# Layer 1's convolution in a four-layer network: six products of 128 columns for four tokens instead of four products of 256 columns for two tokens

## The chip, the cores and the metric

The program runs on one core of a Trainium2 chip. The core has a matrix engine (TensorE, PE in the profile, with its weight loads listed apart as PEld), a vector engine (VectorE, DVE), an engine for activation functions (ScalarE, ACT), a general engine (GpSimd, POOL) and an engine that here does nothing but issue transfers (SyncE, SP). The engines run side by side, each works through its own instructions in the order in which they were put there, and they wait for each other by semaphores. Sixteen DMA engines move data between the device's memory and the core's.

The metric is the time of one execution on the device in microseconds (us). Three runs of the kernel before took 4932.82, 4935.36 and 4935.79 us; the median is 4935.36 us.

## The reference

Two sequences of 1024 tokens with 1024 channels go through four layers, each an attention-like part and a feed-forward part, and after each of these eight parts the input is added and the rows are normalized. All is float32. The change is in the attention part of layer 1, which begins with a convolution over three neighbouring tokens:

```python
x = lax.conv_general_dilated(inputs, conv_w, window_strides=(1,), padding='SAME',
                             dimension_numbers=('NWC', 'WIO', 'NWC')) + conv_b   # 1024 -> 768 channels
q, k, v = jnp.split(x, 3, axis=-1)                # 256 channels each, blocks of 128 tokens
qh = jnp.einsum('btd,dhe->bthe', q, wq) + bq      # 16 heads of 64; kh and vh likewise
scores = jnp.einsum('bqhe,bkhe->bhqk', qh * scale, kh)   # causal within the block
p = jax.nn.softmax(scores, axis=-1)
o = jnp.einsum('bhqk,bkhe->bqhe', p, vh)
o = jnp.einsum('bqhe,hed->bqd', o, wo) + bo
return o.reshape(N, L, W_) @ proj_w + proj_b
```

Written out, the output at token t is W0·x(t−1) + W1·x(t) + W2·x(t+1) + b, with three 1024×768 matrices W0, W1, W2.

## The kernel before, in words

The two sequences (batches) are worked through one after the other, and in each the four layers in turn. `x` holds the rows, `xT` their transposed copy, 8 channel blocks (`k`) of 128 partitions, with one column of zeros ahead of token 0 and one behind token 1023. Weights go through one pool of eight buffers of 128×1024 floats (`self.w()`, tag `w`, 512 KB each); PSUM has eight banks of 512 columns (`self.ps()`).

**The convolution** is done for the two halves `th` of 512 tokens, and in each for six groups `co` of 128 output channels. It uses the identity that yields two neighbouring outputs from four products instead of six. With `j` the number of the product, the moving operand is a sum or a difference of two columns of `xT` (d2+d1, d2−d1, d0−d2, d3−d1), the stationary one is a matrix made of the weights (W0+W1+W2, W0−W1+W2, W0, W2). Each product covers 256 columns (each second token of the half) and sums over 8 channel blocks: 8 matmuls of 128×128 weights and 256 columns. One matmul of float32 stands in the profile as two records, one PEld and one PE each. So a half has 6 × 4 × 8 = 192 matmuls, 384 records, at line 666 (`call(j, k)`).

- `sums(eng, th, ks, outs)`, whose instructions stand at line 631, makes the moving operands. For the first half VectorE does it, into `qh` and `kh` (free until the heads are computed); for the second half GpSimd does it, into the columns of `xT` that the first half no longer needs.
- `load()` at line 647 fetches a group's weights. The made matrices are made only once, in batch 0's first half, by three VectorE instructions on 128×1024 floats (lines 651, 652, 655), and stored to memory (`cvd`, line 657, issued by SP); later they are loaded from there.
- ScalarE copies products 0 with the bias (line 672, `ce`), VectorE adds and subtracts product 1 (line 679, `cf`) and `last()` (line 682) joins these with products 2 and 3 into `qkv`, whose columns of one parity are two apart.

**The first half** of each batch overlaps the end of layer 0: tiles 4 to 7 of `x` still wait for layer 0's feed-forward result, which is loaded from memory as `ys` (line 709) and added by `add_y` (eight PE transposes, line 149; VectorE adds, line 157, and statistics, lines 168 and 169), normalized (`ln_roots`, lines 176 to 188, and `ln_scale`, line 191) and transposed into `xT` by `to_xT` (eight PE transposes, line 135; copies by VectorE, line 102, and ScalarE, line 104, in turn). The order of all this, with groups 0 and 1, is written out by hand in a block `with self.tc.manual_schedule():`, where each engine takes its instructions in the order of the program text. Groups 2 to 5 stand behind that block, and there a scheduler orders the instructions. Then the heads of the first half are computed (`heads(0, ...)`, line 109 in the profile).

**The second half's** convolution is dealt out over the attention of the first half: `attend(calls, per, units)` works on 8 units (4 blocks × 2 groups of heads) in 10 steps, and between the parts of a step it issues `per` entries of the list `calls`, which holds the 192 matmuls, the loads, the joins and eight `add_row` (GpSimd, line 142). `per` is 27.

Of the kernel before, what the change touches and what calls it, by code (L numbers as in the profile page):

```python
# [8 lines left out]
F = mybir.dt.float32  # L9
# [18 lines left out]
class Net:  # L28
# [7 lines left out]
    def __init__(self, ctx, tc, ins, out):  # L36
# [31 lines left out]
        self.cb2 = c.tile([P, 6], F, name="cb2")  # L68
# [523 lines left out]
    def l1_attn(self, b, yd, op):  # L592
        nc, i = self.nc, self.i
        row = self.row("l1_projb")
        with self.tc.tile_pool(name=self.nm("l1a"), bufs=1) as lp, self.tc.tile_pool(name=self.nm("l1s"), bufs=2) as spool:
# [18 lines left out]
            u0 = lp.tile([P, HALF], F, name=self.nm("u0"))  # L614
            cb2 = self.cb2
            if b == 0:
                self.cvd = self.dp.tile([6, 2, P, D], F, name=self.nm("cvd"))
# [5 lines left out]
            def sums(eng, th, ks, outs):  # L623
                v = [
                    self.xT[:, ks, th * HALF + o : th * HALF + o + HALF].rearrange("p k (i s) -> p k i s", s=2)
                    for o in (0, 2)
                ]
                d = [v[j // 2][:, :, :, j % 2] for j in range(4)]
                for j, o in outs:
                    x, y, op = ((2, 1, ALU.add), (2, 1, ALU.subtract), (0, 2, ALU.subtract), (3, 1, ALU.subtract))[j]  # L630
                    eng.tensor_tensor(o, d[x], d[y], op)

            def moving(th, j, k):
                cs = slice(256 * (j % 2), 256 * (j % 2) + 256)
                if th == 0:
                    return (qh, kh)[j // 2][:, k, cs]
                if j // 2:
                    return self.xT[:, k, 1 + cs.start : 1 + cs.stop]
                if k == 0:
                    return u0[:, cs]  # L640
                return self.xT[:, k - 1, 1 + HALF + cs.start : 1 + HALF + cs.stop]

            def conv(th, co):
# [3 lines left out]
                def load():  # L647
                    g = [self.w(i["l1_conv"][co, 0])]
                    if b == 0 and th == 0:
                        g1, g2, t = self.w(i["l1_conv"][co, 1]), self.w(i["l1_conv"][co, 2]), self.w()  # L650
                        nc.vector.tensor_tensor(t, g[0], g2, ALU.add)
                        nc.vector.tensor_tensor(t, t, g1, ALU.add)
                        if co == 0:
                            sums0(0)
                        nc.vector.scalar_tensor_tensor(g1, g1, -2.0, t, ALU.mult, ALU.add)
                        for n, f in enumerate((t, g1)):
                            nc.sync.dma_start(self.cvd[co, n], f)
                        w["w"] = [t, g1, g[0], g2]
                    else:
                        es = [self.w(self.cvd[co, n]) for n in range(2)]  # L660
                        w["w"] = es + g + [self.w(i["l1_conv"][co, 2])]

                def call(j, k):
                    if k == 0 and j % 2 == 0:
                        w["p", j // 2] = self.ps()
                    nc.tensor.matmul(  # L666
                        w["p", j // 2][:, 256 * (j % 2) : 256 * (j % 2) + 256], w["w"][j][:, k * P : (k + 1) * P],
                        moving(th, j, k), start=k == 0, stop=k == KD - 1,
                    )
                    if (j, k) == (2, 1):  # L670
                        w["e"] = spool.tile([P, 256], F, tag="ce", bufs=1, name=self.nm("ce"))
                        nc.scalar.activation(w["e"], w["p", 0][:, :256], AF.Identity, bias=cb2[:, co : co + 1])
                    if (j, k) == (2, 4):
# [20 lines left out]

            c0, c1 = conv(0, 0), conv(0, 1)
            with self.tc.manual_schedule():
                c0[0]()  # L700
                if b:
                    sums0(0)
# [1571 lines left out]
```

## Time and profile before

The table is made from the profile's views by stretch of time; a stage runs from the first to the last of its work on the chain of waits.

| stage | us from the span's start | length | records of line 666 | busy PE | busy VectorE | busy GpSimd |
|---|---|---|---|---|---|---|
| whole program | 0 to 4929.1 | 4929.1 | 1536 | 4529.3 | 3288.3 | 2176.1 |
| batch 0, first half | 294.2 to 407.0 | 112.8 | 384 | 97.78 | 57.94 | 26.84 |
| batch 0, second half, in the attention | 447.6 to 563.2 | 115.6 | 384 | 114.71 | 30.55 | 35.09 |
| batch 1, first half | 2755.6 to 2854.8 | 99.2 | 384 | 92.78 | 35.27 | 19.59 |
| batch 1, second half, in the attention | 2896.0 to 3011.0 | 115.0 | 384 | 114.11 | 30.54 | 35.09 |

The profiled execution took 4930.85 us; its span, from the first instruction of the program to the last, is 4929.1 us. That is 4.5 us below the median of the three timed runs.

How to read it: the four stages with the convolution are 443 us, 9% of the span. In the two second halves PE is busy nearly all the time. In the first halves it is not: there are times at which it waits for VectorE. In batch 0 the made weights are made as well, and that first half takes 13.6 us longer than batch 1's.

### The profile page before, as it was taken

To read this page: it belongs to the slowest core of one execution; us is meant where nothing else is said; L and a number is where in the kernel's file an instruction comes from. 1 tells how busy PE (TensorE), PEld (TensorE's weight loads), DVE (VectorE), ACT (ScalarE), POOL (GpSimd) and SP (SyncE) were. 2 spreads that over 40 slices of the span, in tenths; PEclk is the share of its full clock that TensorE was granted. 3 is DMA by queue.
4 is the path that set the end of the run, shared out by engine and by line. 5 is a ranking of instruction groups with operands and counts; after the bars stand their busy time and mean duration, and the time that the engine had idled before them with its cause. 6 is when DMAs were issued, how large, how long until landed. Compare 5 with 4: busy or idle time off the path is not lost.

```text
span 4929.1 us, 50567 instructions
## 1 busy us (share of the span) xinstructions
PE 4529.3 (92%) x16968; PEld 2231.8 (45%) x16968; DVE 3288.3 (67%) x4421; ACT 2012.2 (41%) x4065; POOL 2176.1 (44%) x1341
## 2 busy tenths in 40 slices
PE   9989989988888888999999999799888988899999
PEld 4357646433333333564443676464333333335644
DVE  5552267399999998545365422653999999976453
ACT  2521232377765654122025212334776756531310
POOL 2132112088888986130021321211888889850310
PEclk9999999999999999999999999999999999999999
DMA  2153212488888999411122532123888899983100
GB/s 92 54 182 131 75 66 90 130 221 228 238 217 230 249 247 248 159 51 48 52 69 63 182 111 71 58 67 122 216 222 236 211 241 256 250 265 120 63 13 30
DMA packets 285256, 723.89 MB, mean 147 GB/s; under 512 B 36928, under 2 KB 87232, under 8 KB 284996
## 3 DMA queue, kind: packets, MB, share of 16 engines
q1 hardware_dynamic: 277316, 695.47, 49.5%
q0 software_dynamic: 7680, 25.17, 1.5%
q8 instruction: 136, 2.23, 0.2%
q14 instruction: 124, 1.02, 0.1%
HBM read 607.00 MB, written 94.63 MB: 142 GB/s over the span
## 4 chain that ended last, share of the span: by engine, by line
PE 55%; DVE 18%; DMA 10%; issue 4%; POOL 4%; ACT 3%; SPq 1%; DVEq 0%; POOLq 0%; ACTq 0%
PE ps L109 15%; DVE h L1385 9%; PE ps L666 6%; PE ps L1757 4%; PE ps L2067 4%; DMA h<-dxd 3%; PE ps L1493 3%; POOL h L1371 2%; PE ps L1770 2%; DVE h L1396 2%; PE ps L1711 2%; PE ps L1407 2%; PE ps L135 2%; PE ps L1378 2%; DMA xi<-xcd 1%
## 5 line engine op out<-in xcount | busy, mean ns | idle before, releaser
L1371 POOL TENSOR_TENSOR h<-h,br 128x1024 f32<-128x1024 f32 x512 | 1205.5, 2370 | 106.6 <-DMA h<-dxd 63.7
L1378 PE MATMUL ps<-hl,rep 128*128 128x512 f32 x1024 | 731.9, 719 | 180.5 <-DVE h L1385 144.6
L1380 ACT ACTIVATE ps<-ps,l_Alog 128x512 f32<-128x512 f32 x1024 | 662.3, 662 | 550.7 <-PE ps L1378 548.0
L1385 DVE TENSOR_TENSOR_SCAN h<-ps,hst,h 128x512 f32<-128x512 f32 x512 | 633.9, 1284 | 20.8 <-ACT ps L1380 17.6
L1396 DVE TENSOR_TENSOR h<-h,ps 128x1024 f32<-128x1024 f32 x512 | 617.3, 1206 | 1.5 <-ACT hst L1393 1.4
L1385 DVE TENSOR_TENSOR_SCAN h<-ps,h 128x512 f32<-128x512 f32 x512 | 599.0, 1211 | 18.8 <-ACT ps L1380 18.8
L1493 PE MATMUL ps<-xT,w 128*128 128x512 f32 x1024 | 548.3, 622 | 8.8 <-DVE h L1385 7.6
L1378 PEld LDWEIGHTS ps<-hl,rep 128*128 128x128 f32 x1024 | 200.9, 197 | 608.3 <-DVE h L1385 436.7
L142 POOL TENSOR_TENSOR x<-x,row 128x1024 f32<-128x1024 f32 x80 | 191.3, 2410 | 548.7 <-PE ps L135 522.5
L1407 PE MATMUL ps<-h,sel 128*32 128x512 f32 x2048 | 294.9, 628 | 5.9 <-DVE h L1396 5.9
L1531 PE MATMUL ps<-w,w 128*128 128x512 f32 x512 | 275.5, 622 | 21.3 <-DMA w<-yd 18.7
L830 POOL TENSOR_TENSOR s<-s,l1r 128x512 f32<-128x512 f32 x64 | 66.5, 1039 | 489.1 <-DVE l1r L829 448.1
L1493 PEld LDWEIGHTS ps<-xT,w 128*128 128x128 f32 x1024 | 190.3, 195 | 203.4 <-issue 166.3
L1316 POOL TENSOR_TENSOR e<-e,one 128x512 f32<-128x512 f32 x64 | 81.5, 1273 | 446.3 <-ACT xp L1188 314.0
L1438 PE MATMUL ps<-xT,w 128*128 128x512 f32 x512 | 271.5, 629 | 6.1 <-DVE h L1385 6.1
L157 DVE TENSOR_TENSOR x<-x,ps 128x512 f32<-128x512 f32 x192 | 128.8, 683 | 216.6 <-PE ps L2073 136.2
L1196 DVE SCALAR_TENSOR_TENSOR ps<-xp,l_convw,ps 128x512 f32<-128x512 f32 x192 | 145.1, 756 | 186.3 <-ACT ps L1191 181.8
L1757 PE MATMUL ps<-w,w 128*128 128x512 f32 x512 | 229.4, 595 | 0.0
L2067 PE MATMUL ps<-w,xT 128*128 128x512 f32 x512 | 225.9, 593 | 0.0
L109 PE MATMUL ps<-xT,w 128*128 128x512 f32 x512 | 225.1, 592 | 0.0
L182 ACT ACTIVATE rs<-mv 128x1 f32<-128x1 f32 (+2 forms) x72 | 14.7, 204 | 473.1 <-DVE mv L176 472.7
L135 PE MATMUL ps<-ident,x 128*128 128x128 f32 x1024 | 140.6, 290 | 58.3 <-DVE x L191 53.4
(300 smaller groups left out, 7748.8 us busy)
## 6 DMA issues: line engine op xcount, KB each, us to landing
h<-dxd SPq DMA_DIRECT2D x512, 512.0 KB, 7.9
w<-l_in SPq DMA_DIRECT2D x128, 512.0 KB, 6.3
w<-l_out SPq DMA_DIRECT2D x96, 512.0 KB, 8.3
w<-l_conv SPq DMA_DIRECT2D x54, 512.0 KB, 4.1
w<-cvd SPq DMA_DIRECT2D x36, 512.0 KB, 3.4
w<-l_fw SPq DMA_DIRECT2D x32, 512.0 KB, 6.2
xcd<-xo SPq DMA_DIRECT2D x64, 256.0 KB, 6.2
xi<-xcd SPq DMA_DIRECT2D x64, 256.0 KB, 8.8
```

The source lines that it names most:

```text
L109: self.nc.tensor.matmul(out, lhsT, rhs, start=j == 0, stop=j == n - 1)
L666: nc.tensor.matmul(w["p", j // 2][:, 256 * (j % 2) : 256 * (j % 2) + 256], w["w"][j][:, k * P : (k + 1) * P], moving(th, j, k), start=k == ...
L1371: nc.gpsimd.tensor_tensor(hs[k], hs[k], norms[of(k)[0]][1].unsqueeze(1).to_broadcast([P, 2, HALF]), ALU.mult)
L1378: nc.tensor.matmul(dA[k, m], rep[:, 4 * m + q, :], hl[u, c][:, jj, :], start=True, stop=True)
L1380: nc.scalar.activation(dA[k, m], dA[k, m], AF.Exp, scale=A[:, g : g + 1])
L1385: nc.vector.tensor_tensor_scan(hs[k][:, m, :], dA.pop((k, m)), hs[k][:, m, :], hst[:, g : g + 1] if u else 0.0, ALU.mult, ALU.add)
L1396: nc.vector.tensor_tensor(hs[k], hs[k], norms[of(k)[0]][3].unsqueeze(1).to_broadcast([P, 2, HALF]), ALU.mult)
L1407: nc.tensor.matmul(py[u, c][32 * j : 32 * j + 32, :], self.sel[:, q, :], hs[k - 1 + j // 2][:, j % 2, :], start=False, stop=q == 3,)
L1493: nc.tensor.matmul(p, w["w"][:, k * P : (k + 1) * P], self.xcols(k, u * HALF, HALF), start=k == 0, stop=k == KD - 1)
L1531: nc.tensor.matmul(p, y[:, cc, t * P : (t + 1) * P], wt[:, cc * HALF : (cc + 1) * HALF], start=c2 == 0 and cc == 0, stop=last,)
L1757: nc.tensor.matmul(pa[tt], y[:, cc * HALF + tt * P : cc * HALF + (tt + 1) * P], w[:, cc * HALF : (cc + 1) * HALF], start=c2 == 0 and cc == ...
L2067: nc.tensor.matmul(p, self.xcols(k, tt * P, P), wt[k][:, ns], start=k == 0, stop=False)
```

## The change

The change replaces the identity for two outputs by the one for four: from six products come four neighbouring outputs (where the direct way needs twelve). A product now covers each fourth token of the half, 128 columns; a half has 6 × 6 × 8 = 288 matmuls of 128 columns instead of 192 of 256.

- **Moving operands**: twelve VectorE instructions on 128×1024 floats (or their parts) per half, with operands that lie four columns apart in `xT`; also for the second half, where GpSimd did it before. They go to `qh`/`kh` for the first half, and to `xT`'s first 768 columns and `vh` for the second.
- **Weights**: six matrices per group; products 0 and 5 use W0 and W2 as they are, products 1 to 4 use made matrices. In batch 0's first half they are made by six VectorE instructions per group, each ahead of the product that needs it (`make`), and stored by GpSimd's queue. W0 and W2 are fetched twice there, once for the making (`raw`) and once for products 0 and 5. So that stage issues 5 loads and 4 stores per group (before: 3 and 2), and the other three stages 6 loads per group (before: 4).
- **Loads as buffers come free**: `queue` lists the loads in order, `pump()` issues those whose buffer (the eighth before them) has been given up by an instruction already written, and each product's last matmul calls it.
- **Joining**: per group two ScalarE copies of 128 columns, and on VectorE two instructions of 256 columns and six of 128 columns, the last four behind product 5 (before: one ScalarE copy and two VectorE instructions of 256 columns, one of 512 columns). The factor −1/6 that the identity leaves is put into the scales of the heads, whose instructions stay as many.
- **Order**: the whole first half, groups 2 to 5 too, is now in the hand-written block. In batch 1 groups 0 and 1 go product by product in turn; in batch 0 group 0 comes first, then group 1. The `sums` of the second half are placed behind products of groups 3 and 4. In `attend`, `per` becomes 36, and the list has 288 matmuls.

The diff, cut to its core:

```diff
-            def sums(eng, th, ks, outs):
...
+            def spot(th, j):
+                if th == 0:
+                    t, n = {1: (qh, 0), 2: (qh, 1), 3: (qh, 2), 4: (qh, 3), 0: (kh, 0), 5: (kh, 1), "a": (kh, 2),
+                            "b": (kh, 3), "c": (kh, 2), "e": (kh, 1)}[j]
+                    return t[:, :, n * P : (n + 1) * P]
...
+            def sums(th, steps, k0=0, k1=KD):
...
+                    if m in (1, -1):
+                        nc.vector.tensor_tensor(o, q, p, ALU.add if m > 0 else ALU.subtract)
+                    else:
+                        nc.vector.scalar_tensor_tensor(o, p, float(m), q, ALU.mult, ALU.add)
+            one = [(2, d[2], -4, d[4]), ("a", d[1], -4, d[3]), (1, "a", 1, 2), (2, "a", -1, 2)]
+            two = [(4, d[2], -1, d[4]), ("b", d[1], -1, d[3]), (3, "b", 2, 4)]
+            c_, e_ = ("c", d[2], -1, d[0]), ("e", d[3], -1, d[5])
+            three, five = [(0, "c", 4, 4), (4, "b", -2, 4)], [(5, "b", -4, "e")]
+            def pump():
+                while queue and (len(ring) < WB or ring[-WB] in freed):
+                    key, f = queue.pop(0)
+                    ring.append(key)
+                    f()
...
+                def raw():
+                    for name, j, src in (("g0", "r", 0), ("g2", 1, 2), ("t", 2, None), ("n", 3, None), ("g1", 4, 1)):
...
+                def make(j):
+                    if j == 1:
+                        nc.vector.tensor_tensor(w["t"], w["g0"], w["g2"], ALU.add)
+                        nc.vector.scalar_tensor_tensor(w["g0"], w["g2"], 4.0, w["g0"], ALU.mult, ALU.add)
+                    w[j] = w[{1: "g2", 2: "t", 3: "n", 4: "g1"}[j]]
+                    if j < 3:
+                        nc.vector.tensor_tensor(w[j], w["t"], w["g1"], ALU.add if j == 1 else ALU.subtract)
                     else:
+                        nc.vector.scalar_tensor_tensor(
+                            w[j], w["g1"], 2.0 if j == 3 else -2.0, w["g0"], ALU.mult, ALU.add
+                        )
+                    nc.gpsimd.dma_start(self.cvd[co, j - 1], w[j])
+                    if j == 4:
+                        free((th, co, "r"))
...
                 def call(j, k):
+                    if k == 0 and j in (1, 0):
+                        w["p", j == 0] = self.ps()
                     nc.tensor.matmul(
+                        part(j), w[j][:, k * P : (k + 1) * P], spot(th, j)[:, k, :], start=k == 0, stop=k == KD - 1
                     )
+                    if k == KD - 1:
+                        free((th, co, j))
...
+                def early():
+                    w["e"] = spool.tile([P, 256], F, tag="ce", bufs=1, name=self.nm("ce"))
+                    nc.scalar.activation(w["e"][:, :P], part(1), AF.Identity, bias=cb6[:, co : co + 1])
+                    nc.scalar.copy(w["e"][:, P:], part(3))
+                def middle():
+                    f = spool.tile([P, 4, P], F, tag="cf", bufs=2, name=self.nm("cf"))
+                    for n, op in enumerate((ALU.add, ALU.subtract)):
+                        nc.vector.tensor_tensor(
+                            f[:, 2 * n : 2 * n + 2, :].rearrange("p a b -> p (a b)"), w["e"], w["p", False][:, 2 * P :], op
+                        )
...
+                    nc.vector.scalar_tensor_tensor(w["q"][:, 1, :], s4, -0.5, s2, ALU.mult, ALU.add)
+                    nc.vector.tensor_tensor(w["q"][:, 2, :], a1, a3, ALU.subtract)
+                def last():
+                    a1, a3, s2, s4 = w["f"]
+                    nc.vector.scalar_tensor_tensor(a1, part(0), -1.5, a1, ALU.mult, ALU.add)
+                    nc.vector.scalar_tensor_tensor(w["q"][:, 0, :], a3, -0.25, a1, ALU.mult, ALU.add)
+                    nc.vector.scalar_tensor_tensor(s2, part(5), -6.0, s2, ALU.mult, ALU.add)
+                    nc.vector.scalar_tensor_tensor(w["q"][:, 3, :], s4, -2.0, s2, ALU.mult, ALU.add)
...
+            ORDER = (1, 2, 3, 4, 0, 5)
+            def product(co, j):
+                if b == 0 and 1 <= j <= 4:
+                    c[co]["make"](j)
+                c[co]["calls"](j)
+            def root(tt):
+                self.ln_roots([tt])
+                self.ln_scale(tt)
             with self.tc.manual_schedule():
...
+                if b == 0:
+                    c[0]["make"](1)
+                for k0, k1 in ((0, 2), (2, 4), (4, KD)):
+                    sums(0, one, k0, k1)
+                    c[0]["calls"](1, k0, k1)
...
+                else:
+                    product(0, 0)
+                    product(0, 4)
+                    c[0]["both"]()
+                    self.table()
+                    self.add_y(4, ys)
+                    root(4)
+                    product(1, 1)
+                    self.add_y(5, ys)
+                    product(1, 2)
+                    self.to_xT(4)
+                    product(1, 3)
+                    sums(0, [e_] + five)
+                    product(1, 0)
+                    product(1, 4)
+                    c[1]["both"]()
+                root(5)
+                for j in (1, 2, 3):
+                    product(2, j)
+                self.add_y(6, ys)
+                for co in (0, 1):
+                    product(co, 5)
+                    c[co]["last"]()
...
+                later = {
+                    (3, 2): [lambda: self.to_xT(7)], (3, 3): [lambda: sums(1, [c_] + one)], (3, 5): [lambda: sums(1, two)],
+                    (4, 2): [lambda: sums(1, [e_])], (4, 4): [lambda: sums(1, three + five)],
+                }
+                for co in (3, 4, 5):
+                    for j in ORDER:
+                        product(co, j)
+                        if j == 0:
+                            c[co]["both"]()
+                        for f in later.get((co, j), []):
+                            f()
+                    c[co]["last"]()
...
-                attend(calls, 27, [(tt, g) for tt in range(4) for g in range(2)])
+                attend(calls, 36, [(tt, g) for tt in range(4) for g in range(2)])
```

`both()` is `early()` and then `middle()`. In the second half `early()` stands behind the first matmul of product 4 and `middle()` behind the third matmul of product 0; `last()` of a group follows the second matmul of the next.

## The prediction

> **What bounds the kernel now.** I read the times of the stages first, then the chain of waits inside them, then the single rows. The chain (start, length, what, how many records) in batch 0:
>
> ```profile
> 351.51 55.49 PE ps L666 x256
> 407.00 41.20 PE ps L109 x96
> ...
> 454.95 10.57 PE ps L666 x48
> 465.51 0.46 PE ps L795 x2
> 465.97 1.09 PE ps L801 x16
> 467.06 2.79 PE ps L666 x12
> 469.85 0.87 PE ps L837 x8
> 470.73 3.89 PE ps L666 x18
> 474.62 1.03 PE ps L848 x16
> ```
>
> Groups 2 to 5 of the first half (256 records) and the whole second half are TensorE alone: no piece of another engine stands between. A unit of attention puts L795, L801, L837 and L848 on that chain, 0.46 + 1.09 + 0.87 + 1.03 = 3.45 us, 27.6 for eight units. So in a second half every matmul record counts. The timeline shows the records' cost:
>
> ```profile
> 448.58 0.97 PEld L801 LDWEIGHTS ps<-kh,qh 64*128 64x128 f32 x16 [0.35 <-issue]
> 448.59 1.16 PE L801 MATMUL ps<-kh,qh 64*128 64x128 f32 x16
> 450.00 3.00 PEld L666 LDWEIGHTS ps<-xT,w 128*128 128x128 f32 x14
> 450.21 3.19 PE L666 MATMUL ps<-xT,w 128*128 128x256 f32 x14
> ```
>
> One 256-column record of L666 lasts 0.38 us, but fourteen take 3.19: (3.19 − 0.38) / 13 = 0.216 us each, the weight load hidden under the record before.
>
> The first half of batch 0 begins in the hand-ordered block, and there VectorE sets the pace:
>
> ```profile
> 308.06 1.23 DVE L651 TENSOR_TENSOR w<-w,w 128x1024 f32<-128x1024 f32 x1 [5.61 <-DMA w<-l_conv]
> 309.32 1.23 DVE L652 TENSOR_TENSOR w<-w,w 128x1024 f32<-128x1024 f32 x1
> 310.58 1.23 DVE L655 SCALAR_TENSOR_TENSOR w<-w,w 128x1024 f32<-128x1024 f32 x1
> 311.73 2.36 DVE L631 TENSOR_TENSOR kh<-xT 128x1024 f32<-128x1024 f32 x2
> 313.00 0.93 PEld L666 LDWEIGHTS ps<-kh,w 128*128 128x128 f32 x3 [5.83 <-DVE kh L631]
> ```
>
> TensorE wants the sums of L631 and has to wait 5.8 us because group 1's weights, which nobody needs yet, stand ahead of them on VectorE. The block keeps the text's order, and each instruction on 128×1024 floats costs 1.23 us.
>
> **The matmuls.** A half has 288 matmuls of two records, 576 records of 128 columns, instead of 384 of 256. The trace has no record with 128×128 float32 weights and 128 columns that is not a transpose. From below: half of 0.216 is 0.108; the transposes of L837 take 0.87 / 8 = 0.109. From above: a load that hides under nothing adds as much again, 0.216. Nearest is L801: ordinary float32 records, 128 columns, loads as wide as the convolution's, in two row groups that work side by side, so sixteen are eight steps: (1.16 − 0.27) / 8 = 0.111. I take 0.112: 576 × 0.112 = 64.5 us per half, against 384 × 0.216 = 82.9.
>
> The Trainium skill speaks against this, "TensorE: Matmul & The Clock Gate": its section "LDWEIGHTS (loading the stationary operand)" puts a load at its columns / 1.2, 107 ns here, "Weight-path perf modes" excludes float32 from fast loads, and "The mechanism" lets a load overlap a running matmul only in another row group. By that rule a record would cost its own 0.108 plus 0.107, and the matmuls would gain nothing: 576 × 0.215 = 124 us per half. The rows of L666 contradict the last part of it, since their loads hide in the same row group; whether one still hides when the matmul is as short as the load, no row shows for 128 rows.
>
> **The second halves** (115.6 and 115.0 us before). TensorE after: 64.5 + 27.6 = 92.1. Beside it lie the joins: VectorE gets 2.4 us per group instead of 1.5 (256 columns 0.34 to 0.41 by L679's row, 128 columns about 0.28 by L428's 0.269; two and six), 14 us in all where it was busy 30 of 115; ScalarE's two copies (L819's kind, 0.37 each) replace one of 0.47. GpSimd's eight `add_row` (2.4 each) run ahead of the attention as before: the first four fill it until about 15 us into the stage, and the weights of unit 1 that stand behind them are needed at 28. Loads: 36 × 0.524 MB = 18.9 MB in 95 us, 199 GB/s, and single slices of the page show 265. Before, 115.6 − 82.9 − 27.6 = 5.1 us were waits and seams, 2.8 of them in the tail behind the last join (VectorE, GpSimd, copy; 558.6 to 563.2 on the chain). With 36 entries per step the list reaches into the last steps and hides some: I keep 3. 92.1 + 3 = 95, **−20 us each, −40 for both**; −16 to −22 with waits between 1 and 5 and a record between 0.109 and 0.116.
>
> **Batch 1's first half** (99.2). No weights are made. Products 64.5, 64 transposes × 0.109 = 7.0. Waits, walked through in the block's order: 4.7 at the start (four sums on two channel blocks, 1.4 us, ahead of the first matmul, then as many and then twice as many ahead of the later ones of product 1), 1.8 until `ys` has landed at 2772.7 (fixed by layer 0's last scatter), 2.0 until tile 7 is normalized: 8.5. VectorE has 65 us of work and is behind TensorE only there. 80 us, **−19**. Six loads in a group's 10.75 us are 293 GB/s; the stretch 2757 to 2773 moved 305, the stretch 312 to 322 363, so the loads stay hidden; without that cover each group costs up to 1.1 us more (3.15 MB at 265 GB/s, 11.9), 6 in all. Range −13 to −21.
>
> **Batch 0's first half** (112.8) is where the change costs. VectorE's own list: making 36 × 1.23 = 44.3; sums of both halves 24 at 1.23, 30.1 with the first four in parts; joins 6 × 2.4 = 14.4; four `add_y` × 2.73 (two adds, two statistics, 0.21); four roots and scales × 2.48; four copies × 0.67. Together 112, against 57.9 now, and it is laid in one order with the products. Column by column:
> - Groups 0 to 2: VectorE works 67.4 us (22.1 making, 15.3 sums, 7.2 joins, 10.9, 9.9, 2.0) and waits six times for a product or a transpose written just ahead of its next instruction (1.9 to 5.2, together 21.3): 88.7.
> - Group 3: 3.7 for `make(1)` (three instructions) while TensorE stands still, 2.4 for the next two, 4.6 waiting for tile 7's transposes, copy 0.7, five sums 6.2, `make(4)` 1.2, 3.6 until product 4 is through, 1.25, three sums 3.7, 1.2: 28.6.
> - Groups 4 and 5: `last()` waits for product 5, and `make(1)` of the next group stands behind it: 3.7 + six products 10.75 + 0.6 + 1.7: 16.8 each.
>
> Sum 151. The 1.7 is the clock: the trace's clock record grants TensorE half speed from 296.7 to 303.5, 310.4 to 317.2 and 330.9 to 334.3, pieces of 3.4 us, each around or behind a wait of 3 us or more (the mean was 0.77 to 312 and 0.74 to 322). Nine of the waits here are longer than that; with half speed for 3.4 us after each the stage is 151, at full speed 137. Two us come on top at the start, because `g1` is now the fifth buffer and so behind a scatter of layer 0 (median 7.4 us to landing). I take 150, **+37**, range +22 to +55.
>
> What else moves there: GpSimd's sums (26.8 us busy) are gone, and 24 stores on its queue at about 1.0 (L499's indirect issues, the nearest row) lie beside nothing. SP issues 30 loads instead of 18 and no stores; each waits for its buffer, and `ys` stands behind the first eight entries, as before. 54 transfers are 28.3 MB in 150 us, 189 GB/s. A group's `g2` may be fetched only once `make(4)` of the group before has read `g0`; it lands 4.1 us later and is needed 8 to 12 us later in groups 3 to 5, some 3 us later in group 2, so it costs at most 2.
>
> **Sum**: −40 − 19 + 37 = −22 on a span of 4929.1: 4907. The timed runs lie 6.3 above the span (median 4935.4), so **4913**.
>
> **Rivals.**
> - *The making hides.* Before, groups 2 to 5 of batch 0 ran without a wait though their weights were made meanwhile. If the block let VectorE make ahead, this half would fall like batch 1's: 113 − 19 = 94, sum −78, 4857. Against: the order shown at 308 to 313. 0.10.
> - *The weight load shows.* Place: every record of a product. If a record takes over about 0.125 us nothing is left: each 0.001 costs 1152 × 0.001 in the second halves and some 0.6 us in the first, 1.8 together, so 22 us are gone at 0.112 + 0.012. At 0.216 the second halves last 155 (+39 each), batch 1's first 135 (+36), batch 0's 200 (+87): +201, 5136. For it: a load's row lasts 0.189 us. Against: L801's loads last 0.188 too (its stretch of 0.97 holds sixteen) and follow each other at 0.11. 0.10.
> - *Batch 0 eats it all*, if its first half takes 162 to 182 by loads that land late: within 10 us of before. 0.13. Beyond 182 slower: 0.08.
>
> **How the numbers follow.** A measurement of this kernel tells 0.2%, 10 us, from no change. The forecast has 0.59, its own range 4890 to 4925 (bounds of the three terms, not all at once). Faster: 0.59 + 0.10 = 0.69; within 0.2%: 0.13; slower: 0.10 + 0.08 = 0.18. The range 4885 to 4942 leaves out most of the first rival and of the second.
>
> **What would show it.** The product line's records start every 0.11 us and last 0.27; the second halves take about 95 us with TensorE alone on the chain; batch 1's first half 80; batch 0's 150, with waits of 4 to 9 us of TensorE that end on VectorE's `w`, and a granted clock under 0.9. I am wrong if the records stand at 0.13 or more, if TensorE waits for loads of `w` (`cvd`, `l_conv`) in batch 1, or if batch 0's first half is under 130.

## The result and the profile after

| | runs | median us | lowest to highest | span of the profiled run |
|---|---|---|---|---|
| before | 6 | 4935.57 | 4932.82 to 4940.27 | 4929.1 |
| after | 6 | 4954.69 | 4948.66 to 4959.43 | 4952.6 |

After to before: 1.0039, 95% interval 1.0027 to 1.0051. The change costs some 19 us; 4913 was predicted, with a range of 4885 to 4942. The result is outside it and on the other side.

Where it went, by stage. A first half is counted from the last transpose of tokens 0 to 511 to the first matmul of the heads, a second half from the last matmul of the heads to the first of the output projection (0.3 us more or less, as the start or the end of that last matmul is taken):

| stage | before | after | measured | predicted |
|---|---|---|---|---|
| batch 0, first half | 112.9 | 166.4 | +53.5 | +37 |
| batch 0, second half | 115.2 | 101.7 | −13.5 | −20 |
| batch 1, first half | 98.9 | 88.3 | −10.6 | −19 |
| batch 1, second half | 115.2 | 101.7 | −13.5 | −20 |
| the four together | 442.2 | 458.1 | +15.9 | −22 |
| all else | 4486.9 | 4494.5 | +7.6 | 0 |

All four signs are as predicted, and all four sizes are off to the bad side. "All else" is code that the change doesn't touch, but 5.9 of its 7.6 us come from the change all the same (see e5); in the six profiles without that effect it takes between 4486.9 and 4507.6 us, so the other 1.7 are not read as an effect. From here on kernels are compared by their stages, and by the timed ratio where there is one.

The stages of after in the view by stretches of time (stretch, length, then busy time and number of records of PE, PEld, VectorE, ScalarE and GpSimd, the granted clock of TensorE, the busy share of the DMA engines, GB/s):

```profile
296.40:462.80 166.40, 99.46 (x641) 96.24 (x642) 113.43 (x161) 8.91 (x26) 14.68 (x25) 0.75 0.54 186
504.00:605.50 101.50, 96.78 (x914) 89.27 (x912) 41.75 (x97) 29.84 (x147) 35.22 (x24) 1.00 0.61 199
2799.70:2888.60 88.90, 78.09 (x645) 76.68 (x644) 71.71 (x125) 17.97 (x34) 1.45 (x1) 0.92 0.73 253
2929.80:3031.20 101.40, 96.74 (x913) 89.19 (x912) 41.74 (x97) 29.78 (x147) 35.21 (x24) 1.00 0.61 199
```

In batch 0's first half VectorE is busy 113 us (57.9 before), and TensorE has a quarter of its clock taken away (granted 0.75; before 0.92). The chain of waits of after shows how the one leads to the other. Where before had 256 records of TensorE in one piece, groups 3 to 5 now read like this (start, length, what, number of records):

```profile
414.35 1.15 DVE w L698
...
415.54 3.80 PE ps L712 x16
...
419.92 0.76 DVE cf L730 x2
...
421.32 1.87 DVE xT L648
423.20 1.88 DVE vh L648
...
425.11 1.23 DVE xT L650
...
427.33 1.23 DVE w L692
...
428.58 1.24 DVE w L693
...
429.84 1.24 DVE w L696
...
431.21 13.71 PE ps L712 x96
...
449.92 12.91 PE ps L712 x96
```

A product waits for its weights (L698); then come VectorE's join (L730), two sums of the second half (L648), a third (L650), and only behind them the three instructions that make group 4's first weights (L692, L693, L696), for which TensorE has been standing still. The 96 records of a whole group then take 13.71 us in place of 96 × 0.112 = 10.75, since the first of them run at half clock, as the stretches of group 4 show (same columns as above):

```profile
431.20:436.90 5.70, 5.69 (x27) 5.70 (x28) 5.67 (x5) 0.00 (x0) 1.59 (x3) 0.50 0.56 195
437.00:444.90 7.90, 7.90 (x71) 7.72 (x70) 4.50 (x7) 0.53 (x2) 0.45 (x1) 1.00 0.97 353
```

It is the order that the prediction described; but the sums that read `xT` with both operands last 1.9 to 2.0 us where it had 1.23.

The second halves have the cadence that was predicted. In the chain of after there:

```profile
522.93 2.68 PE ps L712 x24
525.61 1.02 PE ps L968 x16
526.64 2.00 PE ps L712 x16
...
528.66 0.37 ACT ce L724
529.03 0.17 ACT ce L725
...
529.23 0.94 PE ps L712 x6
```

24 records take 2.68 us, 0.112 each. But two pieces of ScalarE stand on the chain, which had none of it before: the matmuls of product 4 that follow `early` wait for its two copies, in each of the six groups.

### The profile page after: what moved, and what is told of

It reads as the page before. It is cut to its first block, busy times and chain, and to the rows that moved or that the text cites. A ratio compares the mean times of both kernels' runs of the same rounds, so it can differ in the third digit from the quotient of the medians.

```text
span 4952.6 us, 52432 instructions
## 1 busy us (share of the span) xinstructions
PE 4467.3 (90%) x17736; PEld 2217.1 (45%) x17736; DVE 3402.6 (69%) x4626; ACT 2038.6 (41%) x4112; POOL 2147.0 (43%) x1301
## 4 chain that ended last, share of the span: by engine, by line
PE 56%; DVE 20%; DMA 10%; issue 4%; POOL 4%; ACT 4%; SPq 1%; another core or an unknown queue 0%; DVEq 0%; POOLq 0%; ACTq 0%
PE ps L110 16%; DVE h L1510 10%; PE ps L712 5%; PE ps L1882 4%; PE ps L2192 4%; POOL h L1496 3%; DMA h<-dxd 2%; PE ps L1618 2%; DVE h L1521 2%; PE ps L136 2%; DMA dxd<-dx 2%; PE ps L1836 2%; DMA xi<-xcd 2%; PE ps L1895 2%; PE ps L316 2%
## 5 line engine op out<-in xcount | busy, mean ns | idle before, releaser
L1503 PE MATMUL ps<-hl,rep 128*128 128x512 f32 x1024 | 709.8, 697 | 191.6 <-DVE h L1510 163.9
L1618 PE MATMUL ps<-xT,w 128*128 128x512 f32 x1024 | 543.8, 617 | 9.5 <-DVE h L1510 8.3
L1441 POOL TENSOR_TENSOR e<-e,one 128x512 f32<-128x512 f32 x64 | 81.5, 1274 | 438.3 <-ACT xp L1313 315.6
L1563 PE MATMUL ps<-xT,w 128*128 128x512 f32 x512 | 257.5, 600 | 6.1 <-DVE h L1510 6.1
L110 PE MATMUL ps<-xT,w 128*128 128x512 f32 x512 | 225.1, 592 | 0.0
L105 ACT COPY xT<-ps 128x512 f32<-128x512 f32 x128 | 75.6, 592 | 315.9 <-PE ps L136 315.7
L183 ACT ACTIVATE rs<-mv 128x1 f32<-128x1 f32 (+2 forms) x76 | 15.6, 205 | 461.3 <-DVE mv L177 461.0
```

Of the source, the lines that this page charges most:

```text
L110: self.nc.tensor.matmul(out, lhsT, rhs, start=j == 0, stop=j == n - 1)
L1503: nc.tensor.matmul(dA[k, m], rep[:, 4 * m + q, :], hl[u, c][:, jj, :], start=True, stop=True)
L1563: nc.tensor.matmul(p, w["w"][:, k * P : (k + 1) * P], self.xcols(k, u0, HALF), start=k == 0, stop=k == KD - 1)
L1618: nc.tensor.matmul(p, w["w"][:, k * P : (k + 1) * P], self.xcols(k, u * HALF, HALF), start=k == 0, stop=k == KD - 1)
```

## The experiments

Theory: three sizes were wrong for separate reasons (VectorE's instructions in batch 0, ScalarE's copies in the second halves, something in batch 1), and VectorE's written order is what makes batch 0's first half long. Rivals: late loads, stores, the amount of VectorE's work wherever it stands. The stages of all runs, in us, with the ratio to before and its 95% interval where several runs were timed:

| run | b0 first | b0 second | b1 first | b1 second | sum | ratio |
|---|---|---|---|---|---|---|
| before | 112.9 | 115.2 | 98.9 | 115.2 | 442.2 | 1 |
| after | 166.4 | 101.7 | 88.3 | 101.7 | 458.1 | 1.0039 [1.0027, 1.0051] |
| e1, nothing made | 85.0 | 101.7 | 88.6 | 101.6 | 376.9 | one run |
| e2, made ahead | 128.3 | 101.7 | 89.6 | 101.6 | 421.2 | 0.9977 [0.9966, 0.9989] |
| e3, adjacent columns read | 155.8 | 101.7 | 87.5 | 101.6 | 446.6 | one run |
| e4, copies later | 164.2 | 95.9 | 88.5 | 95.9 | 444.4 | 1.0035 [1.0020, 1.0050] |
| e5, e2 + e4 + table | 125.7 | 95.9 | 81.5 | 95.9 | 399.0 | 0.9922 [0.9909, 0.9936] |
| e6, e5 + work on GpSimd | 132.2 | 95.9 | 83.1 | 95.9 | 407.1 | 0.9928 [0.9914, 0.9941] |
| e7, e3 + adjacent columns written | 154.1 | 101.7 | 87.8 | 101.6 | 445.2 | one run |
| e8, waits filled | 160.2 | 101.7 | 88.5 | 101.6 | 452.0 | 1.0043 [1.0029, 1.0057] |
| e9, e5 + sums last | 121.5 | 95.9 | 81.0 | 95.9 | 394.3 | 0.9916 [0.9902, 0.9929] |
| e10, e9 + buffer order | 120.8 | 95.9 | 81.9 | 95.9 | 394.6 | 0.9912 [0.9898, 0.9925] |
| e11, after + buffer order | 166.5 | 101.7 | 88.5 | 101.6 | 458.3 | one run |
| e12, e10 + stores by ScalarE | 125.5 | 95.9 | 81.1 | 95.9 | 398.5 | 0.9918 [0.9903, 0.9933] |

### e1: the weights are not made

```diff
 def make(j):
+    w[j] = w["g0" if j < 3 else "g1"]
+    nc.gpsimd.dma_start(self.cvd[co, j - 1], w[j])
+    if j == 4:
+        free((th, co, "r"))
+    return
```

> Left out: VectorE's 36 instructions that make the weights in batch 0; products 1 and 2 use the raw first tap, products 3 and 4 the raw second one, so the output is not the reference's. Loads, buffers and stores stay as many. Theory (VectorE's one written order of making, sums and joins sets batch 0's first half, 166.4 us): VectorE keeps 113.4 - 36 x 1.22 = 69.5 us of work, about batch 1's 71.7, and the stage falls to 85 to 105 us, batch 1's is 88.9. Rival (loads that wait for their buffers, or the 24 stores, set the pace): the stage stays above 145, with TensorE waiting for w <- l_conv. Batch 1 and the second halves move by less than 1 us by both.

85.0 us, at the low end of the theory's range, against over 145 for the rival. The stretch in e1:

```profile
295.40:380.60 85.20, 76.25 (x641) 74.35 (x642) 71.57 (x126) 9.00 (x26) 14.48 (x25) 0.96 0.99 376
```

The same loads and stores go through in half the time, at 376 GB/s, and the clock stays up. So neither the loads nor the 24 stores made the stage 166 us. With the 44 us of making 81 us go: the rest is waits and half clock that come with where it stands (e2). (Since a waiting load here never waits for a weight to be made, e1 doesn't show that the chain from making to store to next load is free.)

### e2: the same making, earlier in VectorE's order

```diff
...
                 for co in (3, 4, 5):
                     for j in ORDER:
                         product(co, j)
+                        if j in (1, 2):
+                            ahead(co, j + 2)
                         if j == 0:
+                            ahead(co + 1, 1)
                             c[co]["both"]()
+                        if j == 5:
+                            ahead(co + 1, 2)
...
```

`ahead` calls `make` and remembers it, so that `product` doesn't make again; groups 0 to 2 are treated alike.

> Same work; in batch 0 each product's weights are made one or two products ahead of it: the first two of a group before VectorE waits for the joins of the group before, the others one product earlier. Theory (it is the place of the making in VectorE's order, not its 44 us): VectorE's work of 113 us stays, the waits of TensorE on w shrink, the stage goes from 166.4 to 131 to 146 us, the program is 20 to 35 us shorter than the kernel after (4920 to 4935, level with before). Rival 1 (VectorE's amount of work and the joins bound it): above 158. Rival 2 (the buffers come free too late for loads ahead): VectorE waits for w <- l_conv in place of PE, above 158 too, told apart by the releaser that the trace names.

128.3 us and a ratio below 1: 38 us come back without a single instruction less. VectorE is busy 112.96 us, as before the edit. TensorE's products in the stage, in after and in e2 (busy time and mean ns, then idle time ahead of them and what ended it):

```profile
L712 PE MATMUL ps<-qh,w 128*128 128x128 f32 x384 | 68.3, 356 | 67.1 <-DVE w L696 41.1 <-DVE w L698 17.8 <-DVE qh L648 8.2
```

```profile
L712 PE MATMUL ps<-qh,w 128*128 128x128 f32 x384 | 61.6, 331 | 32.4 <-DVE w L696 18.6 <-DVE qh L648 8.2 <-DVE w L698 5.6
```

The waits on made weights (`w`, L696 and L698) go from 58.9 to 24.2 us. The theory holds, with a stage even shorter than its 131 to 146; both its rivals asked for over 158.

### e3 and e7: where the sums read and the joins write

```diff
-d = [x[:, :, :, e] for e in range(4)] + [y[:, :, :, e] for e in (2, 3)]
+d = [self.xT[:, ks, th * HALF + o : th * HALF + o + P] for o in (0, 128, 256, 384, 258, 386)]
```

> The sums read 128 adjacent columns in place of every fourth, so the output is not the reference's; the number and size of all instructions stay. Theory (two operands at a step of 16 bytes cost 2.0 us in place of 1.22): no sum of 128x1024 takes more than 1.3 us; ten of them stand in batch 0's first half, which goes from 166.4 to 157 to 160; batch 1's first half from 88.9 to 83 to 87. Rival (the 2.0 us come from both operands lying in one tile, or from GpSimd on the shared port): they stay at 2.0 and the stages move by less than 1 us.

One group of sums in after, then in e3 (busy time, mean ns):

```profile
L648 DVE TENSOR_TENSOR kh<-xT 128x1024 f32<-128x1024 f32 x3 | 6.0, 1998 | 0.0
L650 DVE SCALAR_TENSOR_TENSOR qh<-kh,qh 128x1024 f32<-128x1024 f32 x2 | 2.5, 1226 | 0.1
```

```profile
L648 DVE TENSOR_TENSOR kh<-xT 128x1024 f32<-128x1024 f32 x3 | 3.7, 1217 | 0.0
```

With both operands at a step of four floats an instruction takes 2.0 us, with adjacent ones 1.22. Six of a half's twelve sums read `xT` so; the other six read the adjacent results of these and take 1.23 at most in after, too (L650 above). In batch 0 that is 10.6 us of the stage (the theory asked for 6 to 9; VectorE's busy time falls by 9, and the granted clock rises from 0.75 to 0.79). In batch 1 it is 0.8 us: there VectorE's sums aren't what TensorE waits for, and the expectation of 83 to 87 failed by a little.

e7 adds adjacent writes: `w["q"]` is rearranged as `"p (s i) -> p s i"`.

> e3 with the joins' results written to adjacent columns of qkv, too, in place of every fourth; the output is not the reference's. Theory (a write at a step of 16 bytes costs 0.39 us in place of 0.28, and a part of that is on batch 0's path): L736, L737, L746 and L748 take 0.27 to 0.30 each, batch 0's first half loses another 1 to 3 us against e3's 155.6, the second halves less than 1. Rival (0.39 is the price of two operands from SBUF): they stay at 0.39 and nothing moves.

L736, L737, L746 and L748 go from 0.39 to 0.29 us, and the stage loses 1.7 more, as the theory said. L736 in e3, then in e7:

```profile
L736 DVE SCALAR_TENSOR_TENSOR qkv<-cf 128x128 f32<-128x128 f32 x6 | 2.3, 391 | 0.2
L736 DVE SCALAR_TENSOR_TENSOR qkv<-cf 128x128 f32<-128x128 f32 x6 | 1.8, 293 | 0.2
```

### e4: ScalarE's copies behind the tile's last product

```diff
-if (j, k) == (4, 0):
+if (j, k) == (0, 0):
     cs.append(early)
```

> In the second halves ScalarE's two copies (L724, L725) are put after the last product of their PSUM tile, behind the first matmul of product 0, in place of after the first matmul of product 4, which writes the same tile. Theory (product 4 waits for the copies because it writes the tile that they read): TensorE's idle time ended by ACT ce disappears (6 waits, about 11 us summed in the two halves), each second half goes from 101.4 to 95 to 98 us, the program 7 to 13 us shorter than the kernel after. Rival (something else, the attention's or the joins' waits, takes their place): the halves stay within 1.5 us of 101.4.

Both second halves take 95.9 us, 5.8 less, and this line of after's list of TensorE's waits in the first of them (us in total, times, longest) is gone:

```profile
PE ps L712 <- ACT ce L725: 4.4, 6, 1.1
```

So the stage stands where the prediction had put it, at 95. The timed ratio shows nothing of the 13.7 us that the stages lost, and the 7 to 13 us by which the program was to be shorter failed to come: all else took 4507.0 us in this profile (4494.5 in after's), and the interval is 15 us wide. In e5 the gain shows in the ratio, too.

### e5: e2 and e4, and the table set in batch 1

```diff
 if b:
+    nc.scalar.copy(self.small([P, 1], "tb"), qh[:, 0, 0:1])
     self.table()
     self.add_y(4, ys)
```

In the trace of after, ScalarE's timeline in batch 1 has a table load between the logarithm (L183) and the exponential (L184) of each root:

```profile
2823.32 0.20 ACT L183 ACTIVATE rs<-mv 128x1 f32<-128x1 f32 x1 [21.27 <-DVE mv L177]
2823.54 1.28 ACT L184 ACT_TABLE_LOAD   x1
2824.84 0.20 ACT L184 ACTIVATE rs<-rs 128x1 f32<-128x1 f32 x1
```

`table()` is there to load one set that serves both. In batch 1 it is now the first thing that ScalarE has in the block, and its load is missing from the trace, which has 16 table loads at L183 and L184 in all; before had none on these two instructions. With a small copy ahead of `table()`, the load is back and the 16 are gone.

> The kernel after with the making ahead (e2), the later copies (e4), and in batch 1 one small ScalarE copy ahead of the preload of the table set, which keeps that preload in the program; in batch 1's first half this last edit alone acts. Theory (four table loads of 1.28 us between Ln and Exp stand on VectorE's path there): that half goes from 88 to 82 to 85 us; with 128 in batch 0's first half and twice 92 in the second halves the program takes 4900 to 4912 us, ratio to before 0.993 to 0.996. Rival 1 (VectorE's amount of work or the start of the stage bounds batch 1's first half): it stays above 87. Rival 2 (what the stages save comes back as half-clock pieces in the layers that are not changed): the stages fall as said and the program stays above 4917.

In e5:

```profile
2751.18 1.28 ACT L199 ACT_TABLE_LOAD   x1
2771.69 0.20 ACT L183 ACTIVATE rs<-mv 128x1 f32<-128x1 f32 x1 [19.22 <-DVE mv L177]
2771.92 0.20 ACT L184 ACTIVATE rs<-rs 128x1 f32<-128x1 f32 x1
```

Batch 1's first half takes 81.5 us, 6.8 less than after's and just under the 82 to 85 of the theory. (Nothing else in e5 touches it; four loads of 1.28 us are 5.1, and the granted clock there is 0.96 in place of 0.92.)

Only eight of the 16 loads lie in that half. The other eight lie behind batch 1's second half, outside the four stages:

```profile
3109.87 0.20 ACT L183 ACTIVATE rs<-mv 128x1 f32<-128x1 f32 x1 [3.47 <-DVE mv L177]
3110.09 1.28 ACT L184 ACT_TABLE_LOAD   x1
3111.38 0.20 ACT L184 ACTIVATE rs<-rs 128x1 f32<-128x1 f32 x1
```

From the first matmul of the output projection to the next preload of the set, batch 1 takes 153.8 us in before, 159.7 in after and 159.8 to 160.6 in the seven runs whose traces have the 16 loads, too; in the five without them (e5, e6, e9, e10, e12) it takes 153.7 to 154.5. In batch 0, where the preload stays, this stretch takes 153.1 to 154.6 in all fourteen. So the missing preload costs 5.9 us more there.

All three edits add up, and e5 is faster than both kernels, by a little more than its forecast of 4900 to 4912. Rival 2, that the gain comes back as half clock elsewhere, is out.

### e6: part of VectorE's work on GpSimd

The edit in short:

```diff
-nc.vector.tensor_tensor(w["t"], w["g0"], w["g2"], ALU.add)      # groups 2 to 5
+nc.gpsimd.tensor_tensor(w["t"], w["g0"], w["g2"], ALU.add)
-nc.vector.tensor_tensor(w[2], w["t"], w["g1"], ALU.subtract)
+nc.gpsimd.tensor_tensor(w[2], w["t"], w["g1"], ALU.subtract)
...
+(3, 3): sums(1, [c_], eng=nc.gpsimd); (3, 4), (3, 0), (3, 5): three sums more
```

> e5 with 12.1 us of VectorE's instructions moved to GpSimd in batch 0: the first sum of taps and the weights of product 2 for groups 2 to 5 (8 instructions of 1.22 us), and in both batches four of the second half's sums (2.0 us each). Theory (with the order mended, the amount of VectorE's work bounds batch 0's first half: 113 of e2's 128 us are busy): about 95 us of work are left and the stage takes 108 to 117 us; program 4885 to 4902. Rival (GpSimd's instructions of 2.4 us and more come late, or hold back the stores behind them and with those the buffers): the stage stays above 124, with TensorE or VectorE waiting for POOL w or for loads.

The theory (108 to 117) fell: the stage takes 132.2, more than e5's 125.7. The rival's waits are there (products that wait for POOL w, 1.3 us at 397.4), but there is a second reason, in the timeline of e6 around two joins:

```profile
366.55 2.79 DVE L741 SCALAR_TENSOR_TENSOR qkv<-cf 128x128 f32<-128x128 f32 x1
366.72 2.36 POOL L701 TENSOR_TENSOR w<-w,w 128x1024 f32<-128x1024 f32 x1
...
392.87 4.75 DVE L741 SCALAR_TENSOR_TENSOR qkv<-cf 128x128 f32<-128x128 f32 x1
393.05 2.02 POOL L648 TENSOR_TENSOR vh<-xT 128x1024 f32<-128x1024 f32 x1
395.02 2.34 POOL L701 TENSOR_TENSOR w<-w,w 128x1024 f32<-128x1024 f32 x1
```

VectorE's L741 (L736 in after) lasts 0.39 us alone, 2.79 beside one GpSimd instruction and 4.75 beside two: its own time and all of theirs. An instruction taken off VectorE for 1.22 us holds it up for 2.4 when it runs beside such a join. The Trainium skill says as much in "SBUF — State Buffer", section "Who interferes with whom": a VectorE instruction with two SBUF inputs contends with a GpSimd instruction that reads SBUF, and the shared pair of ports is locked, not divided. 0.39 + 2.36 against 2.79 agrees.

### e8: TensorE kept busy in its waits

```diff
 def product(co, j):
...
+    for _ in range(fill):     # 4 to 32 by the wait's length, nine products
+        nc.tensor.matmul(p[:, :P], self.ident, self.ident, start=True, stop=True)
     c[co]["calls"](j)
```

> The kernel after, with matmuls of the identity by itself (128 columns, two records each, into a PSUM tile that nobody reads) in TensorE's nine longest waits on VectorE in batch 0's first half, 148 of them, each wait filled to about 2.5 us by its length in the trace of after. The waits themselves stay. Theory (the granted clock halves after waits of 3 us and more, and the products that follow run at half speed on the path; TensorE's records of L712 there last 92 us in place of 64.5): the pieces of half clock get fewer, from 41 us of lost clock to under 20, and the stage goes from 166.2 to 148 to 158 us. Rival (half speed hides behind VectorE, whose order sets the end anyway): the lost clock falls, the stage stays above 162.

160.2: between the two. The stretch in e8:

```profile
298.30:458.50 160.20, 124.76 (x937) 121.31 (x938) 114.16 (x161) 9.00 (x26) 14.54 (x25) 0.87 0.59 201
```

The granted clock of the stage goes from 0.75 to 0.87, the lost clock from 0.25 × 166.4 = 41.6 to 0.13 × 160.2 = 20.8 us, and 6.2 us of the stage come back. The rest of the clock that was given back shows nowhere in the stage, whose end VectorE's order would then set.

### e9 to e12: what bounds the mended version

e9 moves the second half's sums behind group 5 (the edit in short):

```diff
-(3, 3): sums(1, [c_] + one), (3, 5): sums(1, two), (4, 2): sums(1, [e_]), (4, 4): sums(1, three + five)
+(5, 3): sums(1, [c_] + one), (5, 4): sums(1, two + [e_])      # and behind last(5): sums(1, three + five)
```

> e5 with the sums of the second half moved behind the products of group 5 (and the last three behind its join), where VectorE has no weights left to make; before, they stood among the making of groups 4 and 5. Theory (in e5 17 us of sums and 7.3 of making per group fall together in groups 3 and 4, where TensorE needs 10.8 per group): TensorE's waits of 6.7 and 4.4 us in group 4 go, batch 0's first half falls from 125.4 to 106 to 115 us, the heads' matmuls behind it stay within 2 us of 41.2, and the program takes 4878 to 4892. Rival (VectorE's amount of work, 113 us with the transposes' copies, is the bound wherever the sums stand): the stage and the heads together save less than 4 us.

121.5, with the heads unchanged at 41.1: 4.2 us in place of the 10 to 19 that were expected. The rival's "less than 4" is as near, though its reason fails: VectorE is busy 99 of 121 us there, so it isn't full. TensorE still waits 4 to 6 us at the seams of the groups, and VectorE waits 15.4 us ahead of L692 (1.0 in e5):

```profile
294.10:415.60 121.50, 87.54 (x641) 84.68 (x642) 99.27 (x149) 8.89 (x26) 14.78 (x25) 0.85 0.74 256
...
L692 DVE TENSOR_TENSOR w<-w,w 128x1024 f32<-128x1024 f32 x6 | 7.3, 1222 | 15.4 <-DMA cvd<-w 9.2 <-PE ps L712 6.2
```

e10 takes the buffers in another order, to have the raw taps earlier; e11 does only that to the kernel after:

```diff
-(("g0", "r", 0), ("g2", 1, 2), ("t", 2, None), ("n", 3, None), ("g1", 4, 1))
+(("g2", 1, 2), ("g0", "r", 0), ("t", 2, None), ("g1", 4, 1), ("n", 3, None))
```

> e9 with the buffers of a group of raw weights taken in another order: g2, g0, t, g1, n in place of g0, g2, t, n, g1, so that no load of a raw tap takes the buffer that the last weights made for the group before still need. Theory (in e9 TensorE's waits of 4 to 6 us at the seams of groups 1 to 5 come from g2, which is fetched only after the fourth weights of the group before are made, and VectorE then waits 6 to 9 us ahead of L692): L692's wait of 15.4 us in all falls under 4, batch 0's first half from 121.3 to 104 to 114 us, the program to 4878 to 4892. Rival (VectorE's 113 us of work are the bound now, whatever the loads do): L692's wait goes to VectorE's other instructions, the stage stays above 118.

> The kernel after with this order of buffers alone. Theory (in the kernel after it is the making's place in VectorE's order that TensorE waits for; the loads are there in time but for the first group, whose g1 is fetched as third in place of fifth): batch 0's first half goes from 166.2 to 162 to 166 us. Rival (late raw taps are a part of its 53 us): below 158.

e11: 166.5, half a microsecond above the theory's range and far from the rival's 158. In the kernel after the raw taps aren't what is late: the list of waits of that stage has no load in it for TensorE or VectorE. e10: 120.8, which is the rival's number, and L692's wait remains, in the table of groups of e10:

```profile
L692 DVE TENSOR_TENSOR w<-w,w 128x1024 f32<-128x1024 f32 x6 | 7.3, 1219 | 12.2 <-DMA cvd<-w 6.9 <-issue 5.2
```

It names the stores, as the larger part of e9's did. And in e10's list of waits, the queue that issues the loads (us in total, times, longest):

```profile
SPq L86 <- DMA cvd<-w: 79.6, 15, 11.3
```

The loads wait there until the stores of the weights that their buffers held have landed. e12 issues those stores from ScalarE in place of GpSimd.

> e10 with the 24 stores of the made weights issued by ScalarE (busy 9 of 166 us in the kernel after's stage) in place of GpSimd. Theory (in e10 the loads on SP stand 79.6 us in 15 waits behind the landing of stores from GpSimd's queue, and VectorE's L692 then waits for the raw taps): SP's waits on the stores fall under 55 us, L692's wait of 12.2 us under 5, batch 0's first half from 120.6 to 106 to 115 us, the program to 4873 to 4888. Rival (what counts is when the weights are made and how long a store of 0.5 MB lasts, not whose queue it stands in, or VectorE's 113 us of work are the bound): the stage stays above 118.

125.5: the rival's number again. By their ratios e9, e10 and e12 can't be told apart; each is 0.8 to 0.9% faster than before, and e10 has the lowest median of all runs, 4891.03 us against 4940.20 of before on the same chip. SP's waits on the stores fell only to 61.4 us, L692's wait stayed at 12.8, and VectorE's join (L730) now waits 5.5 us for ScalarE's copies (0.0 in e10). What holds the stage at 121 us, when batch 1's takes 81, stays open: the chain from making to store to buffer to load to making is the likely cause, but no run here took it apart. A ninth buffer in the pool, the plain test, wasn't tried.

## Why the prediction was wrong

**The record's cost: right.** 0.112 us per record of 128 columns with 128 rows of weights, in both batches. The rule that the prediction set against it (Trainium skill, "TensorE: Matmul & The Clock Gate", "LDWEIGHTS (loading the stationary operand)" and "The mechanism") would have made 0.215. "The mechanism" also names a background weight buffer as a second way to overlap, which the prediction left out; the cadence fits that one.

**"The second halves … I keep 3": the first size that failed.** The prediction took ScalarE's two copies as two for one beside TensorE, and asked only for their 0.37 us. They read a PSUM tile that product 4 is still writing, so TensorE waits for them: 5.8 us per half (e4), 11.6 of the 13 us by which the two halves fell short. Without that wait the stage is 95.9, the prediction's 95.

**"Waits, walked through in the block's order: … 8.5": the second.** It left out what ScalarE does to its tables once nothing stands ahead of `table()`. 6.8 us (e5); with the load back, the stage is 81.5, the prediction's 80. The same missing load cost 5.9 us more behind batch 1's second half, where the prediction had no change at all.

**"Sums of both halves 24 at 1.23": the third.** That price came from rows with a step of two floats; the prediction carried it over to a step of four without a bound. It cost 10.6 us in batch 0 (e3), and with the joins' writes at the same step, priced at 0.28 and measured at 0.39, 12.3 (e7), out of 16.5 by which that half was longer than predicted; e7's 154.1 stands against 150. The four that are left aren't split up, but the prediction's own sum, 151 and two more at the start, makes 153; it took 150.

**The half clock** was priced at 14 us (151 against 137), as half speed for 3.4 us behind each of nine waits. The number of waits above 3.4 us, nine, came out as stated. The length didn't: two of the three pieces that the prediction lists for before last 6.8 us, not 3.4, and in after's clock record ten pieces of 6.8 or 10.2 us begin within the waits. Groups 4 and 5 lose 3.0 and 2.2 us to them on the chain (13.71 and 12.91 against 10.75), where the sum had 1.7. Filling the waits halved the lost clock and brought 6.2; how much the other half holds wasn't measured.

**Batch 0's order** was seen rightly: making, sums and joins in one line on VectorE, TensorE idle for it. What the prediction didn't weigh is how little binds the making to its place. e2 takes 38 us out of the stage by placing the same instructions earlier; that alone turns the change into a small gain (0.9977).

Together: the forecast was a sum of −22, so 22 us of error turn its sign. Three terms, with no allowance for what the change makes different in them (the shared tile, the first instruction in a block, the step), were short by 11.6, 12.7 (6.8 in the stage and 5.9 behind it) and 12.3 us; these 37 us alone carry it across. The rival that went this way, "batch 0 eats it all", had the right place (166.4 lies in its 162 to 182) but the wrong mechanism: loads that land late. No wait of TensorE or VectorE in that stage ends on a load, and e1 and e11 speak against it; that its range holds the measured stage is luck, and its "within 10 us of before" was off, too.

## What to carry to other kernels

An engine that works in a written order needs its instructions placed by when their result is wanted: look for work that stands right ahead of its user with nothing but a habit to keep it there, and move it ahead of the engine's next wait. A price from the nearest row holds only for the same operand steps, the same tile and the same neighbours; where a change alters one of these, give the term a bound on the bad side. And after any edit that reorders ScalarE, count the table loads in the trace.

## What was not expected of the hardware

- Two float32 operands at a step of 16 bytes: 1.98 to 2.04 us for 128×1024, against 1.22 with adjacent ones (e3) and 1.22 at a step of 8 bytes (L631 before). A result of 128×128 written at 16 bytes: 0.39 against 0.29.
- A VectorE instruction with two operands from SBUF that starts beside a GpSimd `tensor_tensor` ends only after it: 2.79 us in place of 0.39 (e6).
- A matmul into a free part of a PSUM tile waits for ScalarE's read of another part, 0.6 to 1.1 us each time in after. Whether the program's bookkeeping or the chip asks for that wait, the runs don't tell apart.
- The part of the program outside the four stages took 4486.9 to 4507.6 us in the six profiles with the table preload in place, so an edit worth 10 us is seen in its stage, and only sometimes in the time.
